# First pair's block sums moved ahead of GpSimd's tensor operations, some of VectorE's work in another order, weight sums loaded in two transfers each

## The chip, the core and the metric

The kernel runs on one core of one Trainium2 chip. The metric is the device time of one execution in microseconds (us), given as the median of several runs. The core has five engines that run their own instruction queues side by side: TensorE (PE in the profile, its weight loads PEld), VectorE (DVE), ScalarE (ACT), GpSimd (POOL) and SyncE (SP), which here only issues transfers. An engine takes its instructions strictly in order; a wait of one instruction holds all that stand behind it on that engine.

## The reference

32 sequences of 128 tokens with 512 features pass through a block with two halves. `m` selects masked tokens (about an eighth of all); all matrices are float32.

```
emb = silu(t) @ ada_w + ada_b;   shift, scale, gate = split(emb)      # per sequence
norm = layernorm(x) * (1 + scale) + shift, zero where not m
x = x + gate * where(m, gelu(norm@ssm_w1+b1)@ssm_w2+b2 + gelu(norm@bwd_w1+b1)@bwd_w2+b2, 0)
shift, scale, gate = split(silu(t) @ ffada_w + ffada_b)
h = gelu_tanh((layernorm(x) * (1 + scale) + shift) @ ff_w1 + ff_b1)   # 512 -> 1024
out = x + gate * (h @ ff_w2 + ff_b2)                                  # 1024 -> 512
```

## The kernel before

**First half (0 to about 84 us of the profile).** Masked tokens are gathered into 512 slots; the first half is computed for these alone and written to a buffer of rows in DRAM (`x1_rows`).

**Second half (from 84 us).** The 32 sequences are worked off as four *pairs* p = 0 to 3 of two *sides* with four sequences (512 tokens) each. x is loaded per side, the rows that the first half changed are put over it by indirect gathers on GpSimd (`take_first_half`, L885), VectorE makes the layer norm (`Statistics`: batch-norm statistic L917/L918, variance plus epsilon L922 on VectorE, the root L923 on GpSimd; `normalised` L929 and a 32x32 block transpose L1479), transfers turn the blocks, ScalarE scales and shifts.

**First matmul of the second half (`FirstProduct`).** Instead of 8 block products, a pair's matmul is made with 7 products of block sums, in the way of Strassen and Winograd, and each of the 7 is once more cut into 7. The outer products run in the order 1, 2, 5, 6, 3, 7, 4 (`STREAMS`); each has the inner products P1 to P7. In this text 6.P3 is inner product P3 of outer product 6; one such *phase* is four 128x256 matmuls (L1117). Outer products 5, 6, 7 and 4 need sums:

- of tokens: `token_sums(j, n)`, for j = 1 to 4 and four parts n each, on VectorE (L1046 for j = 1, L1050 for 2, L1053 for 3, L1056 for 4). Parts 0 to 2 are 128x512 elements, part 3 is 128x256. Outer product 5 reads the sums j = 1, outer product 6 those of j = 2.
- of weights: made once and kept in DRAM (`t_rows`, seven blocks of 256 columns per partition for each of four sums) and loaded anew for every pair by `load_weights(j)` on SP's queue (L1063). Blocks 0 to 3 belong to P1, P5, P2 and P3, blocks 4 to 6 to P6, P7 and P4.

Each outer product has two PSUM banks, e and a. `phase` issues a phase's matmuls and what follows: after P5, ScalarE copies e to SBUF (L1131); after P1, `seed` adds an earlier result to the bank (L1161 on VectorE, L1163 on ScalarE for the first and the fifth); after P6, VectorE writes e from a (L1142) before P3 may add to it; after P7 and P4, VectorE writes results to SBUF (L1147, L1152) so that P4 may go on. GpSimd adds partial results in SBUF (`with_p5` L1168, `after` L1197, `late_sum` L1201); it never touches PSUM. ScalarE makes the gelu (L1079) or a plain copy (L1175).

**Second matmul (`SecondProduct`, L1304).** One level of seven products in 14 steps (`ORDER`: P1U, P5U, P1V, P5V, and so on for two halves U and V of the tokens); P5 reads sums of hidden blocks (`first_block`, L1251). Its first steps are mixed with the last phases of the first matmul: P1U, 4.P3, 4.P7, P5U, 4.P4, P1V, P5V. `fw2_of.combine` (L394) makes the second matmul's weight sums once, during pair 0. `fb2_step` (L1433) is the difference of the two halves of the last bias.

**Order.** All queues stand in the order in which the program issues; the order is written by hand. For pair 0 the first outer products are listed one by one before the loop (`now.do(...)`). From then on `window(new, old, fill)` issues new.P5, new.P1, old.P3, old.P7, new.P2, new.P6, old.P4, and after the n-th of these the work that `put(w, n, f, ...)` has placed in window w (w counts through `STREAMS`; w = 1 is new = 2, w = 2 is new = 5, w = 3 is 6, w = 4 is 3, w = 5 is 7, w = 6 is 4). So `put(3, 4, ...)` is work behind 6.P2.

Of the kernel before, what the change touches and what calls it, by code (L numbers as in the profile page):

```python
# [14 lines left out]
ALU = mybir.AluOpType  # L15
# [7 lines left out]
def kernel(  # L23
# [49 lines left out]
    nc = tc.nc  # L73
    B, S, D = x.shape
    P = 128
    assert S == P
    G = 4
# [499 lines left out]
    for key, vec in (("ssm1", ssm_b1), ("bwd1", bwd_b1), ("ff1", ff_b1)):  # L577
        n = vec.shape[0] // P
# [78 lines left out]
    fb2 = const.tile([P, D], F32, name="fb2")  # L657
# [50 lines left out]
    t_rows = dram.tile([4, P, 7, 2 * P], F32, name="t_rows")  # L708
# [165 lines left out]
    fb2_step = const.tile([P, D // 2], F32, name="fb2_step")  # L874
# [7 lines left out]
    def take_first_half(p, xs, which=range(2 * G)):  # L882
        for i in which:
            b = 2 * p * G + i
            nc.gpsimd.indirect_dma_start(  # L885
                out=xs[i // G][i % G // 2][:, i % 2],
                out_offset=None,
                in_=x1_rows,
                in_offset=bass.IndirectOffsetOnAxis(ap=slot_i[:, b : b + 1], axis=0),
                bounds_check=NS - 1,  # L890
                oob_is_err=False,
            )
# [131 lines left out]
    class FirstProduct:  # L1024
# [33 lines left out]
        def load_weights(self, j):  # L1058
            side = j % 2 == 0
            if j < 3:  # L1060
                t = gp.tile([P, G, D], F32, tag=f"g{side:d}", name=f"tw_{self.p}_{side:d}", bufs=1)
                self.tw[side] = t.rearrange("p g (h f) -> p (g h) f", f=QT)
            nc.sync.dma_start(self.tw[side][:, :7], t_rows[j - 1])  # L1063


        def place(self, quarter, c):
# [335 lines left out]
    now = FirstProduct(0, of_x[0].cut(), of_w)  # L1402
    now.load_weights(1)
    x_of[1][1] = load_side(1, 1)
    now.load_weights(2)
    for n in range(2):
        now.token_sums(1, n)
    now.apart(1)
    now.do(1, "P1")
    now.seed(1)  # L1410
    now.do(2, "P1")
    now.do(1, "P5", "P2", "P6")
    now.do(2, "P5")
    now.seed(2)
    now.do(1, "P3")
    now.with_p5(2, "12")
    now.do(1, "P7")
    now.with_p5(2, "22")
    take_first_half(1, x_of[1], range(G))
    for n in range(2, 4):  # L1420
        now.token_sums(1, n)
    now.do(2, "P2", "P6")
    for n in range(4):
        now.token_sums(2, n)
    now.do(1, "P4")
    now.token_sums(3, 0)
    for p in range(NP):
        more_pairs = p + 1 < NP
        xs = x_of[p]
        fills = {}  # L1430

        def put(w, n, f, *args):
            fills.setdefault(w, {}).setdefault(n, []).append(lambda: f(*args))  # L1433

        if p:
            for n, at in enumerate(((1, 3), (1, 4), (1, 6))):
                put(*at, now.token_sums, 2, 1 + n)
            put(1, 6, now.token_sums, 3, 0)
        for n, at in enumerate(((2, 1), (2, 3), (2, 3))):
            put(*at, now.token_sums, 3, 1 + n)  # L1440
        for n, at in enumerate(((2, 4), (2, 4), (2, 6), (2, 6) if more_pairs else (3, 1))):
            put(*at, now.token_sums, 4, n)
        put(3, 6, now.load_weights, 3)
        if p == 0:
            put(3, 6, load_rows_of_fw2, 0)
            put(6, 2, fw2_of.combine, 0)
            put(6, 5, fw2_of.combine, 1)
        put(4, 6, now.load_weights, 4)
        if p == 0:
            put(4, 6, load_rows_of_fw2, 1)  # L1450
        second = SecondProduct(p, now.h, xs)
        if p == 0:
            put(
                2, 0, nc.vector.tensor_tensor,
                fb2_step, fb2[:, D // 2 :], fb2[:, : D // 2], ALU.subtract,
            )
        put(6, 0, now.late_gelu, "11")
        put(6, 1, second.seed, 0)
        put(6, 3, second.first_block, 0, 0, 2)
        put(6, 6, second.first_block, 0, 2, 4)  # L1460
        put(5, 4, now.late_sum, "11")
        put(6, 4, now.late_gelu, "12")
        put(6, 5, now.late_gelu, "22")
        put(6, 6, now.late_sum, "21")
        if more_pairs:
            x_next = x_of[p + 1]
            stats = [Statistics(x_next[side], f"{p + 1}_{side}") for side in range(2)]
            xn, xT = {}, {}

            def blocks(side, i):  # L1470

                if i == 0:
                    xn[side] = in_turned_blocks(
                        group_of_tiles(f"{p + 1}_0")
                        if side == 0
                        else sp.tile([P, G, D], F32, tag="s12", name=f"xn_{p + 1}_1")
                    )
                t = stats[side].normalised(i, xn[side][:, :, i])
                nc.vector.transpose(t, t)  # L1479

            def to_feature_rows(side, *queues):
                xT[side] = new_xT(p + 1, side)
                turned(xn[side], xT[side], queues)

            if p:
                put(1, 6, take_first_half, p + 1, x_next, range(G))
            put(2, 6, take_first_half, p + 1, x_next, range(G, G + 2))
            put(3, 4, take_first_half, p + 1, x_next, range(G + 2, G + 3))
            put(5, 4, take_first_half, p + 1, x_next, range(G + 3, 2 * G))
            for i, at in enumerate(((3, 1), (3, 3), (3, 4), (3, 6))):  # L1490
                put(*at, stats[0].one, i)
            put(*((3, 6) if p else (5, 4)), stats[0].root)
            for i, at in enumerate(((4, 4), (4, 6), (5, 3), (6, 4))):
                put(*at, stats[1].one, i)
            put(6, 4, stats[1].root)
        for w in range(1 + (p == 0), 7):
            now.window(STREAMS[w], STREAMS[w - 1], fills.get(w, {}))
        second.load_gate(0)
        second.step(0)
        now.late_gelu("21")  # L1500
        if more_pairs:
            for i in range(2):
                blocks(0, i)
        now.do(4, "P3")
        second.seed(1)
        now.do(4, "P7")
        second.first_block(1, 2, 4)
        if more_pairs:
            blocks(0, 2)
        second.step(1, late=True)  # L1510
        now.do(4, "P4")
        if more_pairs:
            blocks(0, 3)
            to_feature_rows(0, nc.sync)
        second.load_gate(1)
        second.first_block(1, 0, 2)
        second.seed_and_second_block(0)
        fill = {5: [lambda: second.third_block(0)], 7: [lambda: second.third_block(1)]}

        def put(step, f, *args):  # L1520
            fill.setdefault(step, []).append(lambda: f(*args))

        if p == 0:
            put(2, fw2_of.combine, 2)
            put(6, fw2_of.combine, 3)
        if more_pairs:

            for i in range(G):
                put(2 + i // 2, blocks, 1, i)
            for k in range(KC):  # L1530
                put(4 + k // 2, lambda k: scaled(2 * (p + 1), xT[0], k), k)
                put(7 + k // 2, lambda k: scaled(2 * (p + 1) + 1, xT[1], k), k)
                if k == 1:
                    put(4, to_feature_rows, 1, nc.sync, nc.sync, nc.sync, nc.scalar)

            def begin(j):
                if j == 1:
                    of_x[p + 1] = TokenBlocks(p + 1, (xT[0], xT[1]))
                of_x[p + 1].one(j)

            put(8, begin, 1)
            put(9, begin, 2)
            put(9, begin, 3)
            put(10, begin, 4)

            def next_product():
                nxt["p"] = FirstProduct(p + 1, of_x[p + 1].cut(), of_w)
                nxt["p"].load_weights(1)

            nxt = {}  # L1550
            put(10, next_product)
            put(11, lambda: nxt["p"].do(1, "P5", "P1"))
            for n in range(4):
                put(11 + n // 2, lambda n: nxt["p"].token_sums(1, n), n)
            put(13, lambda: nxt["p"].token_sums(2, 0))
            if p + 2 < NP:
                x_of[p + 2] = [[], []]
                put(11, lambda: x_of[p + 2][0].extend(load_side(p + 2, 0)))
            put(12, lambda: nxt["p"].do(1, "P2", "P6"))
            put(13, lambda: nxt["p"].load_weights(2))  # L1560
            if p + 2 < NP:
                put(13, lambda: x_of[p + 2][1].extend(load_side(p + 2, 1)))
        for step in range(2, len(ORDER)):
            second.step(step)
            for f in fill.get(step, ()):
                f()
        if more_pairs:
            now = nxt["p"]
# [11 lines left out]
    with tc.If(more > 0):  # L1580
# [11 lines left out]
        with tc.For_i(0, more, 1):  # L1592
# [12 lines left out]
            for half_no, (mod, was, wbs, bias, bcol, func) in enumerate(  # L1605
# [7 lines left out]
                for j, w in enumerate(was):  # L1613
                    n = FF // len(was)
                    nc.sync.dma_start(wa[:, :, ts(j, n)], w.rearrange("(k p) f -> p k f", p=P))
                for j, w in enumerate(wbs):
                    n = HC // len(wbs)
# [73 lines left out]
```

## Time and profile before

| | |
|---|---|
| median of three runs | 456.7 us (455.54 to 456.86) |
| the profiled execution | 455.45 us, of which 453.7 us are the span of the trace |
| TensorE matmuls | 446.6 us busy (98% of the span), 2151 matmuls |
| VectorE | 331.7 us (73%), 571 instructions |
| ScalarE | 178.0 us (39%) |
| GpSimd | 159.8 us (35%) |
| granted TensorE clock | 0.999 |
| transfers | 70.57 MB, 156 GB/s over the span |

Pair 0's first matmul begins at 83.4 us; the second matmul of pair 0 is mixed in from 124.7 us; the first phase of the next pairs stands at 169.4, 260.6 and about 352 us; the last matmuls are done at 449.4 us. A row of the timeline reads: start in us, busy us, engine, line, operation, output <- input, shape and count, and in square brackets how long the engine had been idle before it and what ended that. A matmul counts as busy from its start to a modelled end, and the next starts before that end, so that the distance between the starts says more than the busy time.

### The profile page before, as it was taken

How to read it: one execution, taken by the hardware profiler on the slowest of the kernel's cores; microseconds unless marked ns; L12 is line 12 of the kernel's file. 1: busy time of each engine (PE TensorE's matmuls, PEld its weight loads, DVE VectorE, ACT ScalarE, POOL GpSimd, SP SyncE). 2: the span in 40 equal slices, each digit the busy share in tenths (PEclk: the TensorE clock that was granted, in tenths of full speed). 3: DMA queues.
4: the chain of work that ended last, by engine and by line, in shares of the span. 5: the costliest groups of instructions: out<-in, count | busy, mean ns of one | idle time of the engine just before them, and what ended most of it. 6: DMA issues, size and time to landing. Idle time of an engine off the chain costs nothing.

```text
span 453.7 us, 6170 instructions
## 1 busy us (share of the span) xinstructions
PE 446.6 (98%) x2151; PEld 370.4 (82%) x2151; DVE 331.7 (73%) x571; ACT 178.0 (39%) x390; POOL 159.8 (35%) x154
## 2 busy tenths in 40 slices
PE   8999999999999999999999999999999999999996
PEld 3884585688888888888888888888888888888885
DVE  5798797697789759886796498867963995534645
ACT  3124127244642552446425514454355154552000
POOL 4220550089770000797700007977000027560000
PEclk9999999999999999999999999999999999999999
DMA  7999449745518817722187167221872442222023
GB/s 251 379 396 407 150 73 326 279 151 172 189 78 180 114 49 251 249 92 82 66 191 107 56 230 264 95 84 54 202 105 59 157 145 82 81 94 93 0 82 107
DMA packets 82611, 70.57 MB, mean 156 GB/s; under 512 B 63112, under 2 KB 63728, under 8 KB 81554
## 3 DMA queue, kind: packets, MB, share of 16 engines
q1 hardware_dynamic: 67762, 58.28, 40.9%
q0 software_dynamic: 4160, 10.54, 6.9%
q10 hardware_dynamic: 10656, 1.33, 2.1%
q8 instruction: 18, 0.29, 0.2%
q14 instruction: 15, 0.12, 0.1%
HBM read 56.46 MB, written 13.70 MB: 155 GB/s over the span
## 4 chain that ended last, share of the span: by engine, by line
PE 92%; DVE 5%; POOL 1%; issue 1%; ACT 1%; DVEq 0%
PE a_o L1304 23%; PE a_m L1117 18%; PE e_o L1304 18%; PE e_m L1117 14%; PE po_s L221 6%; PE ph_s L204 5%; PE ph_s L673 2%; PE pm_ss L309 1%; PE last L1304 1%; PE pm_f L309 1%; PE a_m_alone L1117 1%; PE pl_s L254 1%; DVE xn_sy L1050 0%; PE part_s L333 0%; DVE e_m L1142 0%
## 5 line engine op out<-in xcount | busy, mean ns | idle before, releaser
L1168 POOL TENSOR_TENSOR ha<-p_m,ha 128x512 f32<-128x512 f32 x20 | 25.8, 1289 | 178.8 <-ACT ha L1175 169.2
L1304 PE MATMUL e_o<-fw,ha 128*128 128x256 f32 x256 | 57.9, 379 | 0.0
L939 ACT ACTIVATE xT<-xT,modT 128x128 f32<-128x128 f32 x112 | 44.1, 480 | 31.6 <-DMA xT<-xn 31.4
L1304 PE MATMUL a_o<-t,hb 128*128 128x256 f32 x240 | 54.1, 379 | 0.0
L1304 PEld LDWEIGHTS e_o<-fw,ha 128*128 128x128 f32 x256 | 48.6, 190 | 6.6
L1304 PEld LDWEIGHTS a_o<-t,hb 128*128 128x128 f32 x240 | 45.6, 190 | 6.2
L1079 ACT ACTIVATE hb<-hb,biasT 128x256 f32<-128x256 f32 x64 | 29.0, 500 | 30.4 <-POOL hb L1201 19.8
L1131 ACT COPY p_m<-e_m 128x512 f32<-128x512 f32 x27 | 15.8, 586 | 47.8 <-PE e_m L1117 43.3
L885 POOL DMA_INDIRECT x<-x_rows,slot_i x24 | 29.2, 1218 | 6.0 <-issue 5.3
L1168 POOL TENSOR_TENSOR hb<-p_m,hb 128x512 f32<-128x512 f32 x20 | 29.6, 1481 | 0.3
L1304 PE MATMUL a_o<-fw,ha 128*128 128x256 f32 x128 | 28.9, 379 | 0.0
L1304 PE MATMUL a_o<-t,s 128*128 128x256 f32 x128 | 28.9, 379 | 0.0
L1304 PE MATMUL e_o<-fw,s 128*128 128x256 f32 x128 | 28.9, 379 | 0.0
L221 PE MATMUL po_s<-w,h_s 128*128 128x512 f32 x64 | 28.4, 594 | 0.0
L1175 ACT COPY ha<-e_m 128x512 f32<-128x512 f32 x32 | 18.5, 578 | 24.9 <-PE e_m L1117 24.6
L1304 PEld LDWEIGHTS a_o<-t,s 128*128 128x128 f32 x128 | 24.3, 190 | 3.3
L1304 PEld LDWEIGHTS a_o<-fw,ha 128*128 128x128 f32 x128 | 24.3, 190 | 3.3
L1304 PEld LDWEIGHTS e_o<-fw,s 128*128 128x128 f32 x128 | 24.3, 190 | 3.3
L1142 DVE TENSOR_TENSOR e_m<-a_m,ha 128x512 f32<-128x512 f32 x20 | 13.9, 696 | 17.0 <-POOL ha L1168 6.6
L1079 ACT ACTIVATE ha<-e_m,biasT 128x256 f32<-128x256 f32 x48 | 20.0, 468 | 14.8 <-PE e_m L1117 12.6
L1117 PE MATMUL a_m<-xT,tw 128*128 128x256 f32 x96 | 24.7, 380 | 0.4 <-DVE hb L1147 0.4
L1117 PE MATMUL e_m<-s,fw 128*128 128x256 f32 x92 | 23.8, 381 | 0.0
(237 smaller groups left out, 892.3 us busy)
## 6 DMA issues: line engine op xcount, KB each, us to landing
tw<-t_rows SPq DMA_DIRECT2D x16, 896.0 KB, 5.3
x<-in_x_dram SPq DMA_DIRECT2D x16, 512.0 KB, 8.8
gate<-gate_rows POOLq DMA_DIRECT2D x8, 1024.0 KB, 5.2
out_dram<-x SPq DMA_DIRECT2D x15, 512.0 KB, 4.9
xT<-xn SPq DMA_DIRECT2D x92, 64.0 KB, 2.4
ada_f<-in_L_cond_ffada_w_dram SPq DMA_DIRECT2D x4, 768.0 KB, 13.2
ada_a<-in_L_cond_ada_w_dram SPq DMA_DIRECT2D x4, 512.0 KB
w<-in_L_cond_ssm_w_dram SPq DMA_DIRECT2D x2, 1024.0 KB, 6.2
```

Source lines behind the costliest of these rows:

```text
L204: nc.tensor.matmul(ph[:, :n], w[:, k, ts(f, P)], xT[:, k, :], start=(k == 0), stop=(k == KC - 1))
L221: nc.tensor.matmul(po, h[f][:, ts(i, P)], w[:, f, :], start=(f == 0 and seeded is None), stop=(f == HC - 1), skip_group_check=seeded is no ...
L309: nc.tensor.matmul(pm[ts(j, B), : (hi - lo) * P], sT[:, k, :], kinds[:, k, lo:hi, ts(j, P)], start=False, stop=True, skip_group_check=True,)
L885: nc.gpsimd.indirect_dma_start(out=xs[i // G][i % G // 2][:, i % 2], out_offset=None, in_=x1_rows, in_offset=bass.IndirectOffsetOnAxis(ap= ...
L939: nc.scalar.activation(out, src, AF.Identity, bias=shift, scale=scale)
L1079: nc.scalar.activation(dst[:, n], src[:, n], AF.Gelu_apprx_tanh, bias=biasT[:, f : f + 1])
L1117: nc.tensor.matmul(bank[:, ts(n, QT)], self.w_block(j, product)[:, ts(n, P)], self.x_block(j, product), start=(product in ("P1", "P5") and ...
L1131: nc.scalar.copy(p5, e)
L1142: nc.vector.tensor_tensor(e, a, p5, add)
L1168: nc.gpsimd.tensor_tensor(self.place(RESULT[j], c), self.p5[j], other, ALU.add)
L1175: nc.scalar.copy(self.place(RESULT[j], c), src)
L1304: nc.tensor.matmul(part, src[:, k, ts(i, P)], w[product][:, k, :], start=(last and k == 0), stop=True, skip_group_check=True,)
```

## The change

Three things are changed; no computation is added or taken away.

1. The order before the loop, for pair 0: all four `token_sums(1, n)` and `fb2_step` come before the first phase, and `token_sums(2, 0)` and `(2, 1)` move up to places behind the first phases of outer products 1 and 2.
2. The order within the windows: in pairs 1 to 3 `token_sums(2, 0)` moves from the end of the previous pair's steps to behind 2.P1. The last statistic of side 0 moves from behind 5.P4 to behind 3.P1 and, in pairs 1 and 2, its root with it; the second statistic of side 1 moves from behind 6.P4 to behind 7.P1 (places (3, 6), (4, 6) become (4, 1), (5, 1)); the root of side 1 moves to the end of window 6. In pair 0, the third gather of side 1 moves from (3, 4) to directly behind the second at (2, 6), and the normalisation of the second sequence (`blocks(0, 1)`) moves from before 4.P3 to behind 4.P7.
3. Each load of weight sums becomes two transfers: blocks 0 to 3 (1024 elements per partition) and 4 to 6 (768 elements). SP's queue has 16 more transfers to issue.

The order of the matmuls and of ScalarE's work is unchanged. On GpSimd, the third gather of side 1 in pair 0 stands before L1168 (twice) of outer product 6 and L1197 instead of behind them. The root of side 1 stands behind the last L1201 instead of before it, in pairs 0 to 2; in pairs 1 and 2 the root of side 0 stands behind the two L1168 of outer product 3. On VectorE, where a statistic (L917/L918) stood before a seed (L1161) it now stands behind it. In the changed kernel, lines from 1064 on are higher by one (L1142 becomes L1143, L1161 L1162, L1304 L1305), and those behind the loop's start are lower by a few.

```diff
-            nc.sync.dma_start(self.tw[side][:, :7], t_rows[j - 1])
+            for part in (slice(0, 4), slice(4, 7)):
+                nc.sync.dma_start(self.tw[side][:, part], t_rows[j - 1, :, part])
...
-    for n in range(2):
+    for n in range(4):
         now.token_sums(1, n)
+    nc.vector.tensor_tensor(fb2_step, fb2[:, D // 2 :], fb2[:, : D // 2], ALU.subtract)
     now.apart(1)
     now.do(1, "P1")
     now.seed(1)
     now.do(2, "P1")
     now.do(1, "P5", "P2", "P6")
+    now.token_sums(2, 0)
     now.do(2, "P5")
     now.seed(2)
+    now.token_sums(2, 1)
     now.do(1, "P3")
     now.with_p5(2, "12")
     now.do(1, "P7")
     now.with_p5(2, "22")
     take_first_half(1, x_of[1], range(G))
+    now.do(2, "P2", "P6")
     for n in range(2, 4):
-        now.token_sums(1, n)
-    now.do(2, "P2", "P6")
-    for n in range(4):
         now.token_sums(2, n)
     now.do(1, "P4")
...
         if p:
-            for n, at in enumerate(((1, 3), (1, 4), (1, 6))):
-                put(*at, now.token_sums, 2, 1 + n)
+            for n, at in enumerate(((1, 1), (1, 3), (1, 4), (1, 6))):
+                put(*at, now.token_sums, 2, n)
...
-        if p == 0:
-            put(
-                2, 0, nc.vector.tensor_tensor,
-                fb2_step, fb2[:, D // 2 :], fb2[:, : D // 2], ALU.subtract,
-            )
...
-            put(2, 6, take_first_half, p + 1, x_next, range(G, G + 2))
-            put(3, 4, take_first_half, p + 1, x_next, range(G + 2, G + 3))
+            put(2, 6, take_first_half, p + 1, x_next, range(G, G + 2 + (p == 0)))
+            if p:
+                put(3, 4, take_first_half, p + 1, x_next, range(G + 2, G + 3))
             put(5, 4, take_first_half, p + 1, x_next, range(G + 3, 2 * G))
-            for i, at in enumerate(((3, 1), (3, 3), (3, 4), (3, 6))):
+            for i, at in enumerate(((3, 1), (3, 3), (3, 4), (4, 1))):
                 put(*at, stats[0].one, i)
-            put(*((3, 6) if p else (5, 4)), stats[0].root)
-            for i, at in enumerate(((4, 4), (4, 6), (5, 3), (6, 4))):
+            put(*((4, 1) if p else (5, 4)), stats[0].root)
+            for i, at in enumerate(((4, 4), (5, 1), (5, 3), (6, 4))):
                 put(*at, stats[1].one, i)
-            put(6, 4, stats[1].root)
+            put(6, 6, stats[1].root)
...
-            for i in range(2):
+            for i in range(1 + (p > 0)):
                 blocks(0, i)
         now.do(4, "P3")
         second.seed(1)
         now.do(4, "P7")
+        if more_pairs and p == 0:
+            blocks(0, 1)
         second.first_block(1, 2, 4)
...
-            put(13, lambda: nxt["p"].token_sums(2, 0))
```

## The prediction

> **What bounds the kernel now.** First the page: busy time, then the chain that ended last.
>
> ```profile
> PE 446.6 (98%) x2151; PEld 370.4 (82%) x2151; DVE 331.7 (73%) x571; ACT 178.0 (39%) x390; POOL 159.8 (35%) x154
> ...
> PE 92%; DVE 5%; POOL 1%; issue 1%; ACT 1%; DVEq 0%
> ```
>
> TensorE is the bound: the change adds and removes no matmul, so it can only win back the time in which TensorE stands still. The view of waits (us in total, times, the longest) says on whom its weight loads wait:
>
> ```profile
> PEld e_m L1117 <- DVE e_m L1161: 1.8, 4, 0.5
> ...
> PEld a_m L1117 <- DVE hb L1147: 1.5, 2, 0.8
> ```
>
> These are waits on VectorE, small and few. To size them, the timeline: an undisturbed phase of four 128x256 matmuls starts 0.864 us after the one before; what a phase starts later than that is lost (and the phase after a wait starts another 0.10 late). From 83 us on that gives: 84.45 (0.25), 89.0 (0.26), 99.0 (0.50), 101.75 (0.16), 103.9 (0.41), 133.9 (0.69) in pair 0; 207.6 (0.28), 298.6 (0.28) and 365.35 (0.30) in pairs 1 to 3. The timeline around the middle three:
>
> ```profile
> 91.65 1.01 DVE L1046 TENSOR_TENSOR sx<-xT 128x512 f32<-128x512 f32 x1
> ...
> 92.08 1.71 POOL L1168 TENSOR_TENSOR hb<-p_m,hb 128x512 f32<-128x512 f32 x1
> ...
> 92.58 1.48 DVE L1046 TENSOR_TENSOR sx<-s 128x256 f32<-128x256 f32 x1
> ...
> 97.33 0.41 DVE L1433 TENSOR_TENSOR fb_step<-fb 128x256 f32<-128x256 f32 x1
> ...
> 98.27 0.67 DVE L1147 TENSOR_TENSOR hb<-a_m,hb 128x512 f32<-128x512 f32 x1
> ...
> 99.00 0.73 PEld L1117 LDWEIGHTS a_m<-xT,t 128*128 128x128 f32 x4 [0.63 <-DVE hb L1147]
> ...
> 99.89 2.07 POOL L885 DMA_INDIRECT x<-x_rows,slot_i  x1 [0.30 <-issue]
> ...
> 101.75 0.73 PEld L1117 LDWEIGHTS e_m<-sx,tw 128*128 128x128 f32 x4 [0.29 <-DVE e_m L1142]
> ...
> 102.26 1.83 POOL L885 DMA_INDIRECT x<-x_rows,slot_i  x1 [0.30 <-issue]
> ...
> 103.88 0.73 PEld L1117 LDWEIGHTS e_m<-xn_sy,tw 128*128 128x128 f32 x4 [0.54 <-DVE e_m L1161]
> 104.11 1.28 POOL L1168 TENSOR_TENSOR ha<-p_m,ha 128x512 f32<-128x512 f32 x1
> ```
>
> Two token sums (L1046) run beside GpSimd's first tensor operations and take 1.01 and 1.48 us, where the same forms take 0.68 and 0.41 (start to start 0.60 and 0.34) alone; GpSimd's takes 1.71 instead of 1.27. VectorE is then without a gap from 93.99 to 106, and three results reach TensorE late. The other places:
>
> ```profile
> 131.28 1.27 DVE L929 TENSOR_SCALAR xn<-x,mv,rstd 128x512 f32<-128x512 f32 x1
> ...
> 133.22 0.65 DVE L1147 TENSOR_TENSOR hb<-a_m,hb 128x512 f32<-128x512 f32 x1
> ...
> 133.92 0.73 PEld L1117 LDWEIGHTS a_m<-xT,tw 128*128 128x128 f32 x4 [0.82 <-DVE hb L1147]
> ...
> 137.37 0.65 DVE L1251 TENSOR_TENSOR s<-hb 128x512 f32<-128x512 f32 x1
> ...
> 138.35 1.89 PE L1304 MATMUL e_o<-fw,s 128*128 128x256 f32 x8
> ```
> ```profile
> 206.89 0.68 DVE L1161 TENSOR_TENSOR e_m<-a_m,ha 128x512 f32<-128x512 f32 x1
> ...
> 207.63 0.73 PEld L1117 LDWEIGHTS e_m<-xT,tw 128*128 128x128 f32 x4 [0.41 <-DVE e_m L1161]
> ```
>
> At 133 the result that TensorE wants stands behind two normalisations; the last sum before 138.35 ends at 138.02, so little is spare there. At 207 the seed (L1161) stands behind a batch-norm statistic.
>
> **The change, part by part.**
>
> Sums of pair 0, to 104 us. The four (1,n) sums now start at 84.95 and, at 0.60, 0.60, 0.60 and 0.34, end by 87.2; fb_step (0.41) by 87.5. The next VectorE work waits for TensorE until 88.25, so all this is hidden. (fb_step now stands in front of L1142 and needs the transfer of fb2, issued at 77.4; at the 8.8 us of the page's x loads it is there by 86.2.) The (2,0) sum goes into the gap 88.95 to 89.66, (2,1) into 90.26 to 91.04 (it overlaps GpSimd's start at 90.84 by 0.1). L1142 of product 2 waits for its matmul until 92.77 (start of the phase, 91.70, plus 1.07, as in the rows); the sums (2,2), (2,3), (3,0), (3,1) end by 95.6, and L1147 of product 2 meets its matmul at 97.09 instead of running at 98.27. From there VectorE's queue, at 0.60 for each 512 and 0.34 for each 256: L1142 of 5 at 99.83, its end 100.5 against a phase due at 101.20; the seed of 6 ends at 102.65 against 102.93. All three waits go: 0.50 + 0.16 + 0.41 = 1.07. The waits at 84.45 and 89.0 hang on TensorE's own results and stay. If GpSimd's waits or a dispatch cost 0.1 here, the seed's 0.2 covers most.
>
> The third gather of x's side 1 (GpSimd), moved from 107.99 to right behind the second. L1168 of product 6, two more and L1197 now queue behind it; L1142 of 6, wanted by a phase due at 107.24, waits for L1168, which must start by 105.2. GpSimd reaches its gathers at 93.5 (0.4 earlier, L1168 being 1.27). Here a rule matters. Rows: gathers last 0.99 to 2.07 us, the long ones at 99.89 and 102.26 beside sums L1056. The Trainium skill, "SBUF — State Buffer", section "Who interferes with whom", says that a VectorE instruction with two SBUF inputs holds up a GpSimd instruction that reads SBUF, not one that only writes it; descriptors are written. By the rule seven gathers at 1.0 to 1.3 plus 0.30 each let L1168 start near 104: no loss. By the slowest rows (old durations, the seventh at 2.07) it starts at 105.8: 0.6 lost. I take 104, because the sums now end 0.8 us nearer to 102 and only two gathers were long; 0 to 0.7 stays in the range. In return 1.2 us of GpSimd's queue at 108 goes.
>
> Normalisation of pair 0, 124 to 139, in old times. L1147 of product 4 moves ahead of the second normalisation: by itself that frees 0.69. But GpSimd now does L1201 before the square root, so L1201 runs from 130.14 (when L1251 lets it) to 131.3, and the first L929, ready at 130.3, is held up as the second was at 131.28 (1.27 for 0.53). It ends 0.29 after GpSimd, at 131.6 (as 132.55 followed 132.26). ve (L922, 0.15 to 0.34) is now in this queue too. L1147 then ends at 132.9, before the phase due at 133.34. The remaining queue to the end of the last L1251 is 6.65 long as before without its 0.73 of hold-up, so it ends at 138.25 instead of 138.02, and TensorE, due at 137.66, waits until 138.3 plus 0.1. So only about 0.0 of the 0.69 arrives: the wait moves to the second matmul. If L922 is held up as well, 138.65: a loss of 0.4. I take -0.2.
>
> Pairs 1 to 3. The seed goes ahead of a statistic or (pair 3) of sum (2,0): it can start at 206.08 instead of 206.89, and at 364.0 instead of 364.61. Gain 0.28 + 0.28 + 0.30 = 0.86. What moved behind has no one waiting near: the root's result is read 10 us later, sum (2,0) by product 6. L922 moves into the path of L1147 at 223.0; the phase there is due at 225.0 and covers 0.3, even with the second L929 held up by 0.6.
>
> The split loads. 16 more issues at 0.35 us on SP's queue, which stands waiting most of the time. A rule speaks against it: the same page, section "The DMA setup-cost knee", gives about 2 us fixed to each transfer and asks for the largest possible one; by its fit (2 us + bytes/436 GB/s, an estimate) the second part would land some 2 us later. The trace: the sums were stored as parts of 384 and 512 KB, and from 72 to 76 us these moved 410 GB/s, the engines over 100% busy, no gap between. So I cost 0.35 of issue. The whole load took 4.4 to 6.1 us to land; its first use in product 4 of pair 1 (210.3) had 1.5 spare. The first part now waits only for blocks P1, P5, P2 and P3, leaves earlier and is used first; the second is used 4.3 us later, which covers 2 us also. Cost nothing, gain nothing.
>
> Sum: 1.07 - 0.2 + 0.86 = 1.73, say 1.7 us. The profiled execution took 455.45 (span 453.7 and 1.75 around it): 453.7. The median of the three runs is 1.25 above it, so 456.7 becomes 455.0.
>
> **Rivals.**
>
> GpSimd's queue becomes the wait (same time). Slow gathers start L1168 of 6 at 105.8 and TensorE waits at 6.P3: 1.0 gained, 455.7. For it: the 2.07 and 1.83; against: gathers of 1.00 beside sums at 190.78.
>
> The normalisation costs more (same). If GpSimd's L1201 wins over L1251 at 129.6, VectorE stands 1.1 longer: gain 0.6, 456.1. Against: at 129.56 the square root did not win.
>
> The change leaves VectorE as full as before (nothing): the sums are as many, 331.7 us busy stays but for 1.4. What speaks against it is the 1.5 us of gaps at 87 to 91 that they fill.
>
> Slower: the moved gather waits for its tile. x's last load now stands behind two weight transfers, and POOL reaches the gather at about 102.7 with nine tensor operations behind it. Beyond 1.1 of slack, each us late is lost: slower by 1.4 needs 1.7 + 1.4 + 1.1, a landing at 106.9. Issued at 86.5 with 6.7 to land it is there at 93.2, and the split adds 0.4.
>
> **How the numbers follow.** A measurement here tells about 0.3% (1.4 us) from no change. Forecast 0.55 (own range 454.4 to 455.4); a little more, with the wait at 138 absent too, 0.05: these two make 0.60 faster. Slow GpSimd 0.16, normalisation 0.10, nothing 0.04: 0.30 same. The late gather or another wait in GpSimd's queue 0.10 slower. The range takes in the first rivals and that medians of runs spread by 0.6: 453.7 to 456.5.
>
> **What would show it.** In the profile after: L1046 at 0.68 and 0.41 and the first pair's L1168 at 1.27; no wait at 99, 101.75, 103.9; none at the seeds of pairs 1 to 3; a new wait of the second matmul's P5 near 137 on L1252 (L1251 before); L1168 of product 6 starting before 105.2. PE's busy time stays within 1 us. A wait of that phase of 6.P3 on GpSimd, or a first weight part landing after its use, would make it wrong.

## Result and profile after

The changed kernel took 454.47 us in the median of six runs (454.21 to 455.06), the kernel before 456.69 us in six runs beside them. The ratio is 0.9965 with a 95% interval of 0.9953 to 0.9977: 1.6 us faster, by 1.05 to 2.15. The prediction was 455.0 us, by a gain of 1.7. The time and the sign came out; how the gain is made up did not, as the experiments show.

The profiled execution took 454.21 us with a span of 452.5. The page, busy time and chain, against the two lines shown of before:

```profile
PE 445.4 (98%) x2151; PEld 370.6 (82%) x2151; DVE 334.2 (74%) x571; ACT 178.5 (39%) x390; POOL 158.0 (35%) x154
...
PE 94%; DVE 3%; POOL 1%; ACT 1%; issue 1%
```

VectorE's share of the chain fell from 5% to 3%, although VectorE is busy 2.5 us longer: busy time also counts the time for which an instruction is held up, as the 1.23 us of L922 below. The view of waits (us in total, times, the longest) names two places:

```profile
PEld a_m L1118 <- DVE hb L1148: 1.1, 4, 0.4
...
PEld e_o L1305 <- DVE s L1252: 1.0, 1, 1.0
```

The seeds (L1162; L1161 before) cost 1.8 us before and are no longer near the top. What is late now is the last hidden sum before the second matmul's P5V (L1252), and the result of 6.P7 (L1148) in pairs 1 and 2.

I measure from here on in two ways: by the ratio to the kernel before, run on the same chip beside it, and by the length of the *second half* in the profile, from the start of pair 0's first matmul (L1117, L1118) to the start of the last matmul. The first half, which no kernel here changes, lasted 81.8 to 82.7 us in the profiles of all of them (from the first matmul of all, at 1.25); the second half leaves that spread out. It is 365.57 us before and 364.39 after, 1.18 us less (364.42 in a second profile of the changed kernel). It also leaves out what comes behind the start of the last matmul, and that is not the same in all: 4.75 us in the three kernels with whole loads of weight sums, 4.98 to 5.01 in all with split ones. Why these 0.24 us come with the split is open. Lost time of TensorE is counted as in the prediction, a phase's delay plus the 0.10 of its restart:

| place | before | after |
|---|---|---|
| pair 0, 99.0, 101.75, 103.9 | 0.50, 0.16, 0.41 | 0, 0, 0 |
| pair 0, 4.P4 (133.9) | 0.69 | 0 |
| pair 0, second matmul's P5V | 0 | 0.90 |
| pairs 1 and 2, seed of 3.P3 (207.6, 298.6) | 0.28, 0.28 | 0, 0 |
| pairs 1 and 2, 6.P4 (202.1, 293.0) | 0, 0 | 0.25, 0.22 |
| pairs 1 and 2, 4.P4 (224, 315) | 0, 0 | 0.05, 0.04 |
| pair 3, seed at 365 | 0.30 | 0 |

The columns add up to 2.62 and 1.46, a gain of 1.16.

The timeline of after where the three waits of pair 0 had been:

```profile
101.39 0.42 DVE L1056 TENSOR_TENSOR s<-s,xn_sy 128x256 f32<-128x256 f32 x1
...
101.55 1.12 POOL L885 DMA_INDIRECT x<-x_rows,slot_i  x1 [0.30 <-issue]
...
102.47 0.77 PEld L1118 LDWEIGHTS e_m<-xn_sy,tw 128*128 128x128 f32 x4
...
102.69 1.29 POOL L1169 TENSOR_TENSOR ha<-p_m,ha 128x512 f32<-128x512 f32 x1
```

The last sum takes its undisturbed 0.42 us beside a gather; the weight load that waited 0.54 us for its seed at 103.88 starts at 102.47 without a wait; GpSimd begins its tensor operation only then. The other two places, and first L922 where nothing stands beside it:

```profile
116.40 0.14 DVE L922 TENSOR_SCALAR ve<-mv 128x4 f32<-128x4 f32 x1
...
128.19 1.71 POOL L1202 TENSOR_TENSOR hb<-hb 128x512 f32<-128x512 f32 x1
...
128.70 1.23 DVE L922 TENSOR_SCALAR ve<-mv 128x4 f32<-128x4 f32 x1
...
136.37 0.65 DVE L1252 TENSOR_TENSOR s<-hb 128x512 f32<-128x512 f32 x1
...
137.08 0.94 PEld L1305 LDWEIGHTS e_o<-fw,s 128*128 128x128 f32 x5 [1.03 <-DVE s L1252]
```
```profile
200.14 1.27 POOL L1169 TENSOR_TENSOR hb<-p_m,hb 128x512 f32<-128x512 f32 x1
...
200.34 1.11 DVE L922 TENSOR_SCALAR ve<-mv 128x4 f32<-128x4 f32 x1
...
202.09 0.73 PEld L1118 LDWEIGHTS a_m<-xn_sy,tw 128*128 128x128 f32 x4 [0.38 <-DVE hb L1148]
```

In both, L922, an addition on 128x4 elements that takes 0.14 us at 116.40, stands for over 1.1 us and ends when GpSimd's tensor operation ends (129.93 against 129.90, 201.45 against 201.41). What TensorE waits for is behind it on VectorE.

### The profile page after: what moved, and what is told of

It reads as the page before. It is cut to its first block, busy times and chain, and to the rows that moved or that the text cites. A ratio compares the mean times of both kernels' runs of the same rounds, so it can differ in the third digit from the quotient of the medians.

```text
span 452.5 us, 6201 instructions
## 1 busy us (share of the span) xinstructions
PE 445.4 (98%) x2151; PEld 370.6 (82%) x2151; DVE 334.2 (74%) x571; ACT 178.5 (39%) x390; POOL 158.0 (35%) x154
## 4 chain that ended last, share of the span: by engine, by line
PE 94%; DVE 3%; POOL 1%; ACT 1%; issue 1%
PE a_o L1305 22%; PE a_m L1118 20%; PE e_o L1305 18%; PE e_m L1118 15%; PE po_s L221 6%; PE ph_s L204 5%; PE ph_s L673 2%; PE pm_ss L309 1%; PE last L1305 1%; PE a_m_alone L1118 1%; PE pm_f L309 1%; DVE s L1252 1%; PE pl_s L254 1%; PE part_s L333 0%; DVE xn L929 0%
## 5 line engine op out<-in xcount | busy, mean ns | idle before, releaser
L1169 POOL TENSOR_TENSOR ha<-p_m,ha 128x512 f32<-128x512 f32 x20 | 25.8, 1291 | 179.6 <-ACT ha L1176 169.7
L1305 PE MATMUL e_o<-fw,ha 128*128 128x256 f32 x256 | 57.9, 379 | 0.0
L1305 PE MATMUL a_o<-t,hb 128*128 128x256 f32 x240 | 54.1, 379 | 0.0
L1305 PEld LDWEIGHTS e_o<-fw,ha 128*128 128x128 f32 x256 | 48.6, 190 | 6.6
L1305 PEld LDWEIGHTS a_o<-t,hb 128*128 128x128 f32 x240 | 45.6, 190 | 6.2
L1305 PE MATMUL e_o<-fw,s 128*128 128x256 f32 x128 | 29.0, 380 | 0.6 <-DVE s L1252 0.6
L885 POOL DMA_INDIRECT x<-x_rows,slot_i x24 | 27.2, 1135 | 6.2 <-issue 5.4
L1169 POOL TENSOR_TENSOR hb<-p_m,hb 128x512 f32<-128x512 f32 x20 | 29.2, 1458 | 0.3
L1305 PE MATMUL a_o<-fw,ha 128*128 128x256 f32 x128 | 28.9, 379 | 0.0
L1305 PE MATMUL a_o<-t,s 128*128 128x256 f32 x128 | 28.9, 379 | 0.0
L1305 PEld LDWEIGHTS e_o<-fw,s 128*128 128x128 f32 x128 | 24.2, 190 | 4.3 <-DVE s L1252 1.0
L1305 PEld LDWEIGHTS a_o<-fw,ha 128*128 128x128 f32 x128 | 24.3, 190 | 3.3
L1305 PEld LDWEIGHTS a_o<-t,s 128*128 128x128 f32 x128 | 24.3, 190 | 3.3
L1143 DVE TENSOR_TENSOR e_m<-a_m,ha 128x512 f32<-128x512 f32 x20 | 14.0, 698 | 17.0 <-POOL ha L1169 7.6
L1118 PE MATMUL a_m<-xT,tw 128*128 128x256 f32 x96 | 24.7, 380 | 0.0
L1118 PE MATMUL e_m<-s,fw 128*128 128x256 f32 x92 | 23.7, 380 | 0.0
```

The source lines that it names most:

```text
L885: nc.gpsimd.indirect_dma_start(out=xs[i // G][i % G // 2][:, i % 2], out_offset=None, in_=x1_rows, in_offset=bass.IndirectOffsetOnAxis(ap= ...
L1118: nc.tensor.matmul(bank[:, ts(n, QT)], self.w_block(j, product)[:, ts(n, P)], self.x_block(j, product), start=(product in ("P1", "P5") and ...
L1143: nc.vector.tensor_tensor(e, a, p5, add)
L1169: nc.gpsimd.tensor_tensor(self.place(RESULT[j], c), self.p5[j], other, ALU.add)
L1305: nc.tensor.matmul(part, src[:, k, ts(i, P)], w[product][:, k, :], start=(last and k == 0), stop=True, skip_group_check=True,)
```

## Experiments

All were timed beside the kernel before, in three groups of four, each on one chip: the sums alone, the split, ve on GpSimd and the last root; the changed kernel once more and the roots; the other four. The row "changed" is its first measurement. A second half is that of one profiled execution, a ratio that of several.

| kernel | second half, us | ratio to the kernel before, interval |
|---|---|---|
| before | 365.57 | 1 |
| before, sums of pair 0 alone | 366.20 | 1.0005 (0.9995 to 1.0016) |
| before, split loads alone | 365.27 | 0.9995 (0.9987 to 1.0004) |
| before, sums and the gather | 364.97 | 0.9969 (0.9957 to 0.9980) |
| changed | 364.39 | 0.9965 (0.9953 to 0.9977) |
| changed, once more | 364.42 | 0.9968 (0.9955 to 0.9982) |
| changed, gather back | 365.42 | 0.9984 (0.9973 to 0.9994) |
| changed, normalisation back | 364.52 | 0.9963 (0.9950 to 0.9976) |
| changed, root of side 1 earlier | 363.79 | 0.9955 (0.9936 to 0.9974) |
| changed, root of side 0 later | 363.88 | 0.9955 (0.9942 to 0.9969) |
| changed, both roots | 363.42 | 0.9945 (0.9932 to 0.9957) |
| changed, ve on GpSimd | 364.50 | 0.9983 (0.9969 to 0.9997) |
| changed, root of side 1 last | 367.08 | 1.0043 (1.0030 to 1.0055) |
| both roots, bias copies earlier | 362.98 | 0.9923 (0.9908 to 0.9937) |

### The sums of pair 0 alone

The kernel before with part 1 of the change:

```diff
-    for n in range(2):
+    for n in range(4):
         now.token_sums(1, n)
+    nc.vector.tensor_tensor(fb2_step, fb2[:, D // 2 :], fb2[:, : D // 2], ALU.subtract)
...
+    now.token_sums(2, 0)
     now.do(2, "P5")
     now.seed(2)
+    now.token_sums(2, 1)
...
```

> The kernel before with the new order ahead of the loop alone (the sums and fb2_step of pair 0). My theory (the whole gain of this part comes from VectorE being ahead at 99 us): the waits at 99.0, 101.75 and 103.9 go, 1.06 us; the wait of 0.69 at 133.9 stays and the nine lost quarters at the seeds of pairs 1 to 3 (0.28, 0.28, 0.30) stay: 1.0 to 1.1 us faster than the kernel before. Rival (a win at 104 us is given back at the next wait, since the kernel's later waits hang on VectorE's queue and GpSimd's, which do not start earlier): the wait at 133.9 grows by as much as was won, less than 0.4 us faster.

Measured: nothing won, 0.2 us slower by the ratio (interval from 0.2 faster to 0.7 slower), the second half 0.63 us longer. My expectation failed; the rival's time came, but its way only in part. The waits at 99 and 101.75 went (0.66), but the one at 103.9 grew from 0.41 to 1.03:

```profile
102.12 1.33 POOL L1168 TENSOR_TENSOR ha<-p_m,ha 128x512 f32<-128x512 f32 x1
...
102.23 1.50 DVE L1056 TENSOR_TENSOR s<-s,xn_sy 128x256 f32<-128x256 f32 x1
...
104.39 0.73 PEld L1117 LDWEIGHTS e_m<-xn_sy,tw 128*128 128x128 f32 x4 [1.17 <-DVE e_m L1161]
```

With six gathers in its queue GpSimd reaches L1168 at 102.12, 0.11 us before VectorE's last sum. That sum, two operands in SBUF, takes 1.50 us instead of 0.42, and the seed behind it is late. Further on the wait at 4.P4 grew by 0.33 as well, as the rival has it. So the sums were moved out of one overlap with GpSimd and the last of them into another. Besides, TensorE stops once for 0.39 us, and the row puts that down to a load of weight sums:

```profile
119.50 1.10 PE L1117 MATMUL e_m<-s,tw 128*128 128x256 f32 x4 [0.16 <-DMA tw<-t_rows]
```

This load, in one piece here, was issued at 113.33. The phase was due 5.85 us later, and the last signal of the load's landing came at 119.36, 6.03 after the issue.

### The sums and the gather

The same, with the third gather of side 1 moved in pair 0:

```diff
-            put(2, 6, take_first_half, p + 1, x_next, range(G, G + 2))
-            put(3, 4, take_first_half, p + 1, x_next, range(G + 2, G + 3))
+            put(2, 6, take_first_half, p + 1, x_next, range(G, G + 2 + (p == 0)))
+            if p:
+                put(3, 4, take_first_half, p + 1, x_next, range(G + 2, G + 3))
```

> The kernel before with the new order ahead of the loop, as in the run of the sums alone, and with the third gather of side 1 in pair 0 moved ahead of product 6's two L1168. My theory, formed from the run of the sums alone (there GpSimd was done with six gathers at 102.1 and began L1168, so that the last sum, 128x256, took 1.50 us instead of 0.42 and the seed of product 6 came 1.03 us late): a seventh gather keeps GpSimd away from SBUF until 103.2; the last sum takes 0.42 us, the wait at 103.9 is 0.0 to 0.2 us, and the kernel is 0.9 to 1.3 us faster than the kernel before, of which the sums alone brought nothing. Rival (the gather is indifferent, what is won in pair 0 is given back later whatever is done): the wait at 103.9 may go, but the time is within 0.4 us of the kernel before.

Measured: 1.4 us faster than the kernel before (0.9 to 2.0). No wait from 99 to 104; the last sum takes 0.42 us beside a gather, and L1168 starts later:

```profile
101.61 0.42 DVE L1056 TENSOR_TENSOR s<-s,xn_sy 128x256 f32<-128x256 f32 x1
...
101.77 1.13 POOL L885 DMA_INDIRECT x<-x_rows,slot_i  x1 [0.30 <-issue]
...
102.92 1.28 POOL L1168 TENSOR_TENSOR ha<-p_m,ha 128x512 f32<-128x512 f32 x1
...
385.41 1.10 PE L1117 MATMUL e_m<-s,tw 128*128 128x256 f32 x4 [0.16 <-DMA tw<-t_rows]
```

The second half is 0.60 us shorter, although it holds a stop of 0.39 us at 385 for a weight load (issued at 379.24, landed 6.04 later), as the run before does; the waits at 4.P4 and at the seeds are as before, within 0.06. The theory holds. Nearly the whole gain of the change is in these two edits together, and none of it in the first alone.

### The gather back

The inverse, on the changed kernel (the three lines above taken back).

> The changed kernel with the third gather of side 1 in pair 0 back behind product 6's L1198. My theory: L1169 of product 6 starts 1.3 us earlier and overlaps the last sum (L1056, 128x256), which takes 1.3 to 1.5 us instead of 0.42; the wait at the seed of product 6 is back at 0.8 to 1.1 us, and GpSimd's queue behind 107 is 1.0 us longer. 0.7 to 1.3 us slower than the changed kernel. Rival (my prediction, which costed this move at nothing): within 0.3 us of the changed kernel.

Measured: the second half 1.03 us longer than the changed kernel's, and 0.7 to 0.9 us of its gain gone by the ratios. The last sum is held up again, and the seed of product 6 costs 1.03:

```profile
101.69 1.33 POOL L1169 TENSOR_TENSOR ha<-p_m,ha 128x512 f32<-128x512 f32 x1
...
101.80 1.50 DVE L1056 TENSOR_TENSOR s<-s,xn_sy 128x256 f32<-128x256 f32 x1
```

The other waits are those of the changed kernel to 0.01. My prediction had costed this edit at nothing; it is the largest single term.

### The split loads alone

```diff
-            nc.sync.dma_start(self.tw[side][:, :7], t_rows[j - 1])
+            for part in (slice(0, 4), slice(4, 7)):
+                nc.sync.dma_start(self.tw[side][:, part], t_rows[j - 1, :, part])
```

> The kernel before with each load of weight sums in two transfers, nothing else. My theory (the first use of a weight sum has over 1.5 us to spare, and a part that is needed later goes later): no change, within 0.3 us of the kernel before, and TensorE's waits of the second half as before. Rival A (a transfer costs some 2 us however small, and the second part comes late): slower by 1 us or more, with a wait of PEld on the transfer into tw. Rival B (the split is what brought the gain): faster by 0.5 us or more.

Measured: the same within its uncertainty (0.6 us faster to 0.2 slower). The waits are those of before, but the one at the seed of pair 3 (0.30) is absent. It stands at 0.30, 0.19 and 0.36 in the three profiles with whole loads, so it varies; whether it went by that or by the split, no run here tells apart. The transfers, in the page's list of issues (count, size, median us to landing), first of the kernel before, then of this one:

```profile
tw<-t_rows SPq DMA_DIRECT2D x16, 896.0 KB, 5.3
```
```profile
tw<-t_rows SPq DMA_DIRECT2D x16, 512.0 KB, 4.0
...
tw<-t_rows SPq DMA_DIRECT2D x16, 384.0 KB, 4.0
```

Each part lands sooner than the whole, though the 4.0 of the second part is one landing alone, of a part issued 3.5 us behind its first. Where the second is issued right behind the first (the loads at 172.8, 181.7, 264.0 and 363.9), its last packet ends 0.9 to 1.2 us after the first part's, not 2.

The ratio doesn't show what the split does against the stops at 119.5 and 385 of the two runs above: the kernel before had none in its profile. With whole loads, 5.85 us lie between the issue and the first use in product 4 of pair 0 (112.81 to 118.66 before), with split ones 9.3 (107.99 to 117.29 after), since the first part need not wait for the last blocks to come free. Two of the three profiles with whole loads hold such a stop, none of those with split loads does.

### The roots

Three kernels, run beside the changed kernel itself (median 454.53 us there, against 456.16 of the kernel before).

> The changed kernel once more, unchanged, as the measure for the three kernels beside it. All theories: 0.9965 of the kernel before (0.9953 to 0.9977 in its first measurement), about 454.5 us; the second matmul's P5V waits 0.8 us for L1252 at 137; 6.P4 waits 0.25 us for L1148's result at 202 and 0.22 at 293.

Side 1 earlier:

```diff
-            put(6, 6, stats[1].root)
+            put(6, 4, stats[1].root)
```

> The changed kernel with the root of side 1 back behind 4.P2 (in pairs 0 to 2), so that ve (L922, 128x4 elements) runs before GpSimd's last L1202 and not beside it. My theory (what is left is lost where L922 stands beside a GpSimd tensor operation, 1.23 us instead of 0.14, and the root stands behind L1202): L922 in pair 0 takes 0.14 to 0.2 us, the last L1252 ends 0.6 us or more earlier against TensorE, and the wait of 0.9 us at the second matmul's P5V falls to 0.0 to 0.3 us: 0.6 to 0.9 us faster than the changed kernel, 453.7 us; the waits at 202 and 293 stay at 0.25 and 0.22. Rival (VectorE's queue before P5V is simply too long, whatever the order of the root): the wait at 137 stays at 0.7 us or more and the time is that of the changed kernel within 0.2 us.

Side 0 later:

```diff
-            put(*((4, 1) if p else (5, 4)), stats[0].root)
+            put(5, 4, stats[0].root)
```

> The changed kernel with the root of side 0 behind 7.P2 in all pairs, where it stands in pair 0 already, instead of behind 3.P1 in pairs 1 and 2. My theory (L922, held up beside GpSimd's L1169 for 1.11 us, stands before L1148 of product 6, so that the gain of pairs 1 and 2 was given back there): the waits of 0.25 us at 202 and 0.22 at 293 go, the seeds at 207 and 298 stay without a wait: 0.45 us faster than the changed kernel, 454.0 us. Rival (the statistic of 0.6 us that was moved to the same place is what makes L1148 late): both waits stay at 0.15 us or more, and the time is that of the changed kernel within 0.2 us.

Both:

> Both of these changes together. My theory: the places are 65 us and more apart, so the gains add: 1.1 to 1.4 us faster than the changed kernel, 453.2 us, and no wait of TensorE over 0.3 us is left behind 100 us of the profile. Rival (VectorE is as full as before, a wait that is removed comes back at the next place): less than 0.5 us faster.

Measured, against the changed kernel's 364.42 and 454.53 us: side 1 earlier 0.63 shorter in the second half (median 454.28); side 0 later 0.54 shorter (453.93); both 1.00 shorter (453.46), a little under the 1.1 to 1.4 expected. The intervals of the ratios overlap, so that it is the waits in the profiles that tell these kernels apart. Side 0 later does what was expected, the waits at 202 and 293 are gone and the statistic that stayed there costs nothing. With side 1 earlier the wait at P5V goes, but one of 0.38 that I had not expected appears one step ahead, at P1V. The timeline of the kernel with both:

```profile
128.36 1.46 POOL L923 TENSOR_TENSOR rstd<-ve,half 128x4 f32<-128x4 f32 x1
...
128.87 0.54 DVE L929 TENSOR_SCALAR xn<-x,mv,rstd 128x512 f32<-128x512 f32 x1
...
129.80 1.26 POOL L1202 TENSOR_TENSOR hb<-hb 128x512 f32<-128x512 f32 x1
...
133.26 3.32 PEld L1305 LDWEIGHTS a_o<-fw,ha 128*128 128x128 f32 x16 [0.52 <-ACT a_o L1244]
```

The square root (128x4) lies beside the first normalisation and does not hold it up (0.54 us); the longest L922 of this kernel is 0.30 us. In exchange L1202 runs 1.6 us later, the gelu that needs it too, and ScalarE's bias copy for P1V stands behind that gelu.

### ve on GpSimd

```diff
-            nc.vector.tensor_scalar(ve, self.mv[:, :, 1], EPS, None, ALU.add)
+            nc.gpsimd.tensor_scalar(ve, self.mv[:, :, 1], EPS, None, ALU.add)
```

> The changed kernel with ve (L922, 128x4) computed by GpSimd ahead of its own root, so that VectorE has no such instruction in the second half. It tells what is lost to L922 itself from what any VectorE instruction at that place would lose. My theory (beside a GpSimd tensor operation a VectorE instruction that has all its operands in SBUF is held up, one with an operand in PSUM is not): at 202 and 293 what stands next is L1148 with an operand in PSUM, so both waits go (0.47 us); in pair 0 what stands next is L929, all in SBUF, which now takes 1.2 us beside L1202 instead of 0.54, so the wait at P5V stays at 0.6 to 0.9 us. Together 0.4 to 0.7 us faster than the changed kernel. Rival (L922 alone is the loss, a small instruction is what suffers): the wait at P5V goes as well, 1.2 to 1.4 us faster than the changed kernel.

Measured: the mechanism as expected, the time not. The waits at 202 and 293 are gone, and in pair 0 the wait at P5V stays at 0.70, because the next VectorE instruction takes the place of L922:

```profile
128.72 1.71 POOL L1202 TENSOR_TENSOR hb<-hb 128x512 f32<-128x512 f32 x1
...
129.23 1.49 DVE L929 TENSOR_SCALAR xn<-x,mv,rstd 128x512 f32<-128x512 f32 x1
```

So it is not the small instruction that costs, but the place beside L1202. The expected 0.4 to 0.7 us did not come, the second half being 0.1 us longer than the changed kernel's: ve and the root now follow each other on GpSimd ahead of L1198, and L1143, which needs that, makes TensorE lose 0.44 us at 205.2 and again a pair later.

### The normalisation back

```diff
-            for i in range(1 + (p > 0)):
+            for i in range(2):
                 blocks(0, i)
...
-        if more_pairs and p == 0:
-            blocks(0, 1)
```

> The changed kernel with the normalisation of the second sequence (blocks(0,1)) back before 4.P3 in pair 0. My theory (the end of VectorE's queue at the last L1252 sets the end of this stage in both orders): a wait of 0.7 to 1.0 us is back at 4.P4, where L1148 ends 1.2 us later, and the wait at P5V falls by about as much, to 0.0 to 0.2 us: within 0.25 us of the changed kernel. Rival (the move brings the 0.69 us that its wait at 133.9 measured): both waits add, 0.5 to 0.8 us slower than the changed kernel.

Measured: 1.07 us lost at 4.P4 (PEld waits 1.21 for L1148) and none at P5V; the second half 0.12 us longer than the changed kernel's, the ratios equal within their intervals. The wait moves from one place to the other with little change in size, as the theory has it.

### The root of side 1 last

Side 0 as above, and the root of side 1 behind the last normalisation of side 0:

```diff
-            put(6, 6, stats[1].root)
...
             to_feature_rows(0, nc.sync)
+            stats[1].root()
         second.load_gate(1)
```

> The changed kernel with the root of side 0 behind 7.P2 in all pairs, as in the run with both roots moved, and the root of side 1 still later, behind the last normalisation of side 0: its result is not read before the normalisations of side 1, some 3 us after that. GpSimd then has L1202 ahead of the root, as in the changed kernel, and L922 finds GpSimd idle. My theory: L922 takes 0.14 us; the first L929 of pair 0 stands beside L1202 and takes 1.2 us instead of 0.54, which leaves 0.4 to 0.6 us more in VectorE's queue than with both roots moved, but GpSimd's last L1202 is done 1.4 us earlier and the wait of 0.28 us on ScalarE at 133 goes; the wait at P5V is 0 to 0.3 us. 0.9 to 1.4 us faster than the changed kernel, 453.1 to 453.6 us, and within 0.3 us of the kernel with both roots moved. Rival (the square root beside the normalisation is what the gain with both roots moved hangs on): the wait at P5V is back at 0.6 us or more, 454.0 us.

Measured: 2.0 us slower than the kernel before (1.0043) and 2.7 us longer than the changed kernel in the second half. Both times were missed, though the wait that the rival named came: L922 does take 0.13 us, but the first L929 is held up (1.49) and P5V loses 0.77. Most is lost at the starts of the first matmul of pairs 1 to 3 (3.3 us in all), where VectorE's results are late. GpSimd's queue in pair 0 shows what is late there:

```profile
136.48 1.39 POOL L923 TENSOR_TENSOR rstd<-ve,half 128x4 f32<-128x4 f32 x1 [5.92 <-DVE ve L922]
...
137.84 0.60 POOL L896 DMA_DIRECT2D gate<-gate_rows  x1
```

The load of the second gate tile (L896, 1024 KB) stands behind the root and is issued at 137.84 instead of 133.45 (kernel with both roots), in the middle of the block transfers of x; ScalarE gets its first turned block at 151.03 instead of 148.66, and VectorE's first sums of it (L986) start 2.4 us later. One block transfer takes SP from 140.64 to 143.48 to issue, where those around it take 0.6 to 0.8 us, while the DMA engines move 337 GB/s (140 to 142 us; 84 in the kernel with both roots). That this load is the cause is read from the trace; no run of its own tests it.

### Both roots, bias copies earlier

On the kernel with both roots, `second.seed(1)` (ScalarE's two copies, L1244) ahead of the gelu that waits for L1202:

```diff
+        second.seed(1)
         now.late_gelu("21")
...
         now.do(4, "P3")
-        second.seed(1)
```

> The kernel with both roots moved, and ScalarE's two copies of the bias into the banks of the second matmul's half V (L1244) ahead of the gelu that waits for GpSimd's last L1202. My theory: what is left in that kernel is 0.38 us at P1V, where L1244 stands in ScalarE's queue behind that gelu; ScalarE stands idle from 127.1 to 131.1, L1244 runs there, and the wait goes: 0.2 to 0.4 us faster than the kernel with both roots moved, 453.1 us, 1.4 to 1.8 us faster than the changed kernel. Rival (VectorE's last L1252 is due at the same time and takes the wait over at P5V): no gain over the kernel with both roots moved, 453.5 us.

Measured: median 453.04 us, ratio to the kernel before 0.9923 (0.9908 to 0.9937), second half 0.44 us shorter than with both roots and 1.41 shorter than the changed kernel's. The copies run at 128.34 and 128.87, the wait at P1V is gone, and L1252 costs 0.05 at P5V. This is the fastest kernel of the study. Its page:

```profile
PE 445.2 (99%) x2151; PEld 372.4 (82%) x2151; DVE 330.3 (73%) x571; ACT 178.1 (39%) x390; POOL 158.5 (35%) x154
...
PE 98%; DVE 1%; POOL 0%; issue 0%
```

VectorE has a share of 1% in the chain, and TensorE no wait over 0.05 us after 90 us.

## Why the prediction was right, and where it was not

**The sums of pair 0, +1.07.** 1.07 came, by all three waits, with the sums at 0.68 and 0.42 us and the seed at 101.72. The time was right and the account of it was not: the term was given to the sums, and they bring nothing without the gather.

**The gather, 0 (0 to 0.7 lost).** This is the step that failed. I asked only what the longer queue in front of L1168 could cost, and weighed for that the rule of the Trainium skill, "SBUF — State Buffer", "Who interferes with whom", by which a gather is not held up by VectorE's sums. The seven gathers of after, beside these sums, agree with it: they take 1.00 to 1.28 us, and L1169 starts at 102.69, well before 105.2. The 2.07 and 1.83 of before, which come again as 2.08 and 1.83 in the run of the split alone, do not fit it and stay open. But the same rule read from the other side says that the sums are not held up while GpSimd gathers. My own figures put the last sum just where GpSimd would begin L1168 without the seventh gather: a seed that ends at 102.65 and takes 0.68, with a sum of 0.34 from start to start before it, has that sum start at about 101.6, and six gathers of 1.0 to 1.3 and 0.30 each, from 93.5, end between 101.3 and 103.1 (estimates). Costed so, the move is worth the 1.0 us that the gather's return measured.

**The normalisation, -0.2.** -0.21: 0.69 won at 4.P4, 0.90 lost at P5V. The place was foreseen; that the size fits is luck. L1202 ran earlier than I had it (128.19, not 130.14), so that it held up L922, while the first L929, on which I had put the hold-up, took its 0.54. For the case that L922 is held up as well I had 0.4. The same section of the skill says that the engine which issues first has the shared ports for the whole instruction and the other stands; 1.23 us for 128x4 elements, ending with L1202, agrees. Taking the size of the operation (0.15 to 0.34 us) for its price was the error.

**Pairs 1 to 3, +0.86.** 0.56 of the seeds came, and 0.30 of pair 3, which was gone with the split alone too; 0.56 was lost again at 6.P4 and 4.P4 of pairs 1 and 2: net 0.30. The sentence that failed is "What moved behind has no one waiting near". I thought of who waits for the root's result, 10 us later, and not of what stands behind L922 on VectorE: L1148, which TensorE needs within a microsecond. The run with the root of side 0 later gives 0.54 back.

**The split loads, 0.** 0 within 0.6 us, but not for the reason given. The 1.5 us to spare were read at one load of pair 1; two loads that took 6.0 us stopped TensorE for 0.39 each in the runs above, and no profile with split loads shows such a stop. On the other side stand the 0.24 us behind the last matmul. The rule that I weighed against it did not show: the second part ends 0.9 to 1.2 us behind the first.

**Sum.** 1.07 - 0.21 + 0.30 is 1.16, against 1.73 predicted and 1.18 measured in the second half; the ratio of the times says 1.6 with an interval that holds both. Less the 0.24 behind the last matmul, the profiles account for 0.9 us, a little under that interval. The profiled execution of the kernel before (455.45) was faster than its median in any group (455.75 to 456.69), so that a usual execution may lose more than this profile shows; what, is open. That 1.7 came so near to 1.6 is therefore in part luck: the parts that are accounted for make less. The median of the kernel before, from which the forecast was taken, was the same again (456.69), and the difference of the medians, 2.2, contains the spread of the first half. Of the rivals none came about: the gathers were not slow and the moved one did not wait for its tile. That the change as a whole leaves VectorE as full as it was is true of busy time (334.2 against 331.7 us), and says nothing of the time.

## To carry to other kernels

Where two engines hold each other up, price a move by what will stand beside it at its new time, from the other engine's queue: an instruction of 0.14 us costs 1.2 if it lands beside a tensor operation of GpSimd, and the time of GpSimd's gathers was a place to hide VectorE's sums, which kept their 0.68 and 0.42 us there. Look at what stands behind a moved instruction in its own queue before asking who reads its result. And when a wait goes, follow the next result in line on every engine: here P5V, then P1V behind ScalarE, and the kernel in which a load of 1024 KB stood behind such a wait in GpSimd's queue was the slowest of all.

## What the runs showed of the hardware

- An addition on 128x4 elements (L922) takes 0.14 us alone. Beside a GpSimd tensor operation on 128x512 it ends 0.03 to 0.04 us after that operation: 1.08 to 1.24 us where it starts 0.2 to 0.5 into it, 0.30 where it starts 1.0 into it. Beside a gather it takes 0.32 to 0.35. Size does not protect: the normalisation (L929, 128x512) takes 1.49 beside L1202 and 0.53 alone, a sum of 128x256 with both operands in SBUF 1.50 and 0.42.
- Beside the same GpSimd operations a VectorE addition with an operand in PSUM is not held up (L1161 at 103.65 in the run of the sums alone: 0.68 us beside L1168, as elsewhere), nor is the batch-norm statistic (L917 at 199.41 of after: 0.69 us beside L1169), although all its operands are in SBUF; the theory of the run with ve on GpSimd was too wide there.
- GpSimd's square root on 128x4 elements takes 1.04 to 1.47 us, and the normalisation beside it is not held up (0.54 us).
